# Second feed-forward layer of four batches: tokens sorted by expert in place of all experts for every token

## The chip, the cores and the metric

The kernel runs on one core of a Trainium2 chip. The metric is the device time of one execution in microseconds (us). Engines are named as in the profile: PE is the matrix engine (PEld its weight loads), DVE the vector engine, ACT the scalar engine, POOL the GpSimd engine, SP the engine that here only issues transfers. Everything is computed in f32.

## The reference, cut to what matters

```python
def ffn(x):                                  # x: tokens x 128
    scores = sigmoid(x @ gate_w.T)           # 16 experts
    _, idx = top_k(scores + gate_b, 4)
    w = take(scores, idx); w = w / w.sum(-1) * 2.5
    comb = zeros(T, 16).at[arange(T)[:, None], idx].add(w)
    y = sum(comb[:, e] * (silu_and_mul(x @ w13[e].T) @ w2[e].T) for e in range(16))
    return y + silu_and_mul(x @ w13_s.T) @ w2_s.T     # a shared expert, for every token

x = x + 0.5 * ffn(layernorm(x))
x = x + attention(layernorm(x))              # causal, rotary, one head of 128
x = x + 0.5 * ffn(layernorm(x))              # the same weights again
```

x has 8 batches of 1024 tokens of 128 features. An expert has 64 hidden units (gate and up halves of w13). Of 16 experts each token uses four; the weights in comb of the other twelve are zero.

## The kernel before, in words

The first feed-forward is layer 0, the second is layer 1. The unit of work is a `Group`: 512 tokens (half a batch) in one layer, 32 groups in all. A group computes all 16 experts for all its tokens: two experts make a block k of 128 hidden units, so there are eight blocks.

- Phase U, slots U0 to U8: for each k, `gate(k)` (line 273) and `up(k)` (286) are matmuls with 512 columns into PSUM banks that alternate; ACT applies SiLU (288), DVE multiplies by up (290) into `hidT`, and `weigh(k)` on POOL (294) multiplies by `cb`, the tokens' weights for the block's two experts.
- Phase D, slots D0 to D8: `down(k)` (302), four matmuls of 128 columns for each k, sums up the blocks; `down_shared` (311) adds the shared expert, whose hidden part `Shared.up` computed (336 to 341); `add` (317 to 325) adds half of it to x on DVE, and in layer 1 SP stores the result.

The order of the whole program is written by hand. A table `jobs` says, for every group's period p and each of its 18 slots, what else is put there; all engines get their instructions in that order, and each of them works through its own list in order. Beside group p's own U and D work, there stand in the slots of period p: the preparation of group p + 2 (`norm_a`, `norm_b`, `turn`, `route_a`, `route_b`, `score`, `top_a` to `top_c`: layer norm, transpose on PE, router, top four on DVE, lines 159 to 247), its `spread` (the weights go through DRAM, lines 256 to 266, and come back as `cb`, 2 MB a group, broadcast over 64 partitions), and the attention: for each batch `Heads` (norm, projections, rotary products on POOL, 376 to 394) and eight `Query` steps (`scores` 409, `exp` 420, `turn` 436 to 442, `attend` 448 to 452), two or three of them a period from period 3 to 28.

The group order interleaves the layers: layer 0 of batches 0 to 3, then layer 1 of batch b - 4 and layer 0 of batch b in turn, then layer 1 of batches 4 to 7.

PSUM has eight banks. Banks 0 to 3 serve U, bank 0 the sum of D; `hold` reserves banks for a stretch of slots, and `other_bank()` gives out the rest by age. Tiles in SBUF come from pools with so many buffers for each tag; a tile of which all buffers are in use makes its next writer wait.

Of the kernel before, what the change touches and what calls it, by code (L numbers as in the profile page):

```python
# [9 lines left out]
F32 = mybir.dt.float32  # L10
AF = mybir.ActivationFunctionType
# [4 lines left out]
P = 128  # L16
# [10 lines left out]
def kernel(  # L27
# [11 lines left out]
    rope: bass.AP,  # L39
    out: bass.AP,  # L40
# [16 lines left out]
    xpool = ctx.enter_context(tc.tile_pool(name="xpool", bufs=5))  # L57
    ln = ctx.enter_context(tc.tile_pool(name="ln", bufs=2))
    small = ctx.enter_context(tc.tile_pool(name="small", bufs=3))
# [35 lines left out]
    for n in range(2):  # L95
        bi = const.tile([P, GT, E + TOPK], F32, name=f"biased{n}")
        nc.gpsimd.memset(bi[:, :, E:], PAD)
        biased.append(bi)

# [47 lines left out]
    def stats(key, b, tiles):  # L147

        if key not in mvs:
            mvs[key] = small.tile([P, NT, 2], F32, tag="mv", name=f"mv_{key}", bufs=16)  # L150
        for t in tiles:
            st = small.tile([P, 6], F32, tag="st", name=f"st_{key}_{t}")
            nc.vector.bn_stats(st, xs[b][:, t, :])
            nc.vector.bn_aggr(mvs[key][:, t, :], st)

    def deviation(key, g):
        tiles = slice(g * GT, (g + 1) * GT)
        rstd = small.tile([P, GT], F32, tag="rstd", name=f"rs_{key}_{g}")
        nc.vector.tensor_scalar(rstd, mvs[key][:, tiles, 1], LN_EPS, None, ALU.add)
        nc.gpsimd.tensor_tensor(rstd, rstd, neg_half, ALU.pow)  # L160
        return rstd

    def normed(key, b, g, rstd):
        xn = ln.tile([P, GT, D], F32, tag=f"xn{key[0]}", name=f"xn_{key}_{g}")
        for j in range(GT):
            t = g * GT + j
            nc.vector.tensor_scalar(  # L167
                xn[:, j, :], xs[b][:, t, :], mvs[key][:, t, 0:1], rstd[:, j : j + 1],
                ALU.subtract, ALU.mult,
            )  # L170
        return xn
# [9 lines left out]
    class Group:  # L181
        def __init__(self, layer, b, g, n):
# [14 lines left out]
        def route_a(self):  # L197
# [7 lines left out]
            self.lt = small.tile([P, P], F32, tag="lt", name=f"lt_{self.nm}", bufs=2)  # L205
# [11 lines left out]
        def top_a(self):  # L217
# [3 lines left out]
            self.bi = biased[self.n % 2]  # L221
# [16 lines left out]
        def top_c(self):  # L238
# [3 lines left out]
            tot = small.tile([P, GT], F32, tag="tot", name=f"tot_{self.nm}")  # L242
# [9 lines left out]
        def spread(self, parts=2):  # L252
# [4 lines left out]
            cT = small.tile([P, P], F32, tag="cT", name=f"cT_{self.nm}", bufs=2)  # L257
# [3 lines left out]
            pairs = cd.rearrange("(n h) s -> h n s", h=2)  # L261
            self.cb = big.tile([P, NP, W], F32, tag="cb", name=f"cb_{self.nm}")
            for q in range(parts):
                ns = slice(q * NP // parts, (q + 1) * NP // parts)
                for h in range(2):
                    nc.sync.dma_start(
                        out=self.cb[h * I : (h + 1) * I, ns, :],
                        in_=pairs[h, ns, :].unsqueeze(0).broadcast_to([I, NP // parts, W]),
# [8 lines left out]
        def up(self, k):  # L277

            if k == 0:
                self.hidT = big.tile([P, NP, W], F32, tag="hidT", name=f"hidT_{self.nm}")  # L280
# [11 lines left out]
        def weigh(self, k):  # L292
            hid = self.hidT[:, k, :]
            nc.gpsimd.tensor_tensor(hid, hid, self.cb[:, k, :], ALU.mult)  # L294
# [32 lines left out]
    class Shared:  # L327
# [5 lines left out]
        def up(self):  # L333
            self.h = work.tile([P, W], F32, tag="sh", name=f"sh_{self.pair[0].nm}", bufs=1)
            for n, gr in enumerate(self.pair):
                nc.tensor.matmul(bank(5 - n), ws, gr.hT, start=True, stop=True)  # L336
            for n, gr in enumerate(self.pair):
                s_ps = bank(5 - n)
# [5 lines left out]
                gr.sh = self.h  # L344

    class Heads:
# [5 lines left out]
        def deviations(self):  # L354
# [5 lines left out]
            self.rl = small.tile([P, NT], F32, tag="rl", name=f"rl_{b}")  # L360
# [9 lines left out]
        def project(self, w, g):  # L370
# [4 lines left out]
            p = bank(5 - w)  # L375
# [3 lines left out]
            other = work.tile([P, W], F32, tag="ot", name=f"o_{nm}", bufs=2)  # L379
# [16 lines left out]
    class Query:  # L396
# [6 lines left out]
        def scores(self, first):  # L403
# [10 lines left out]
            top = self.top = small.tile([P, 1], F32, tag="top", name=f"top_{self.nm}")  # L414
# [3 lines left out]
        def exp(self):  # L418
            self.pr = att.tile([P, S], F32, tag="pr", name=f"pr_{self.nm}", bufs=3)
# [39 lines left out]
    LAG = 4  # L459
    order = [(0, b) for b in range(LAG)]  # L460
    for b in range(LAG, B):
        order += [(1, b - LAG), (0, b)]
    order += [(1, b) for b in range(B - LAG, B)]
# [4 lines left out]
    heads = [Heads(b) for b in range(B)]  # L468

# [7 lines left out]
    def when(p, slot):  # L477
        return p * len(slots) + slots.index(slot)

# [13 lines left out]
    queue = [(b, i) for b in range(B) for i in range(NT)]  # L493
    starts, done = {}, {}
    for p in range(3, 29):
        for n in range(2 if p in (15, 21) or (p % 2 == 0 and p != 26) else 3):
            if not queue:
                continue
            b, i = queue.pop(0)
            starts.setdefault(b, p)  # L500
            q = Query(heads[b], i)
            s, first, e, t0, t1, a = (
                ((p, "U7"), 4, (p, "D0"), (p, "D3"), (p, "D5"), (p, "D7")),
                ((p, "D2"), 2, (p, "D5"), (p, "D8"), (p + 1, "U0"), (p + 1, "U2")),
                ((p, "D4"), 4, (p, "D7"), (p + 1, "U3"), (p + 1, "U4"), (p + 1, "U5")),
            )[n]
            at(*s, lambda q=q, first=first: q.scores(first))
            hold((first, first + 1), s, e)
            at(*e, q.exp)
            at(*t0, lambda q=q: q.turn(0))  # L510
            at(*t1, lambda q=q: q.turn(1))
            at(*a, q.attend)
            done[b, i] = when(*a)
    assert not queue
# [3 lines left out]
    for b in range(B):  # L518
        h, st = heads[b], starts[b]
        ready = when(turn_of[0, b, 1] + 1, "U7")  # L520
        if b == 0:
            p0, p1 = st - 1, st - 1
            places = ("U8", "D0", "D2", "D3", "D5", "D6", "D7", "D8")
        else:
            p0, p1 = st - 2, st - 1
            places = ("D0", "D3", "D5", "D8", "U1", "U4", "U5", "U6")
        assert ready < when(p0, places[0])
        at(p0, places[0], h.deviations)
        at(p0, places[1], lambda h=h: h.norm(0))
        at(p0, places[2], lambda h=h: h.norm(1))  # L530
        at(p0, places[3], lambda h=h: h.turn(0))
        at(p1, places[4], lambda h=h: h.turn(1))
        for w in range(2):
            for p, slot, g in ((p1, places[5 + w], 0), (st, ("U4", "U5")[w], 1)):
                at(p, slot, lambda h=h, w=w, g=g: h.project(w, g))
                hold((5 - w,), (p, slot), (p, slot))
        at(p1, places[7], lambda h=h: h.values(0))
# [3 lines left out]
    for p, gr in enumerate(groups):  # L541
        steps = (
            gr.norm_a, gr.norm_b, gr.turn, gr.route_a, gr.route_b, gr.score, gr.top_a, gr.top_b,
            gr.top_c, gr.spread,
        )
        if p == 1:
            steps = steps[1:]
            places = [(0, s) for s in ("U3", "U5", "U6", "U8", "D0", "D1", "D2", "D3", "D6")]
        else:
            places = [(p - 2, s) for s in ("U5", "D1", "D4", "D5", "D7", "D7", "D8", "D8")]  # L550
            places += [(p - 1, "U1"), (p - 1, "U3")]
# [7 lines left out]
        if p % 2 == 0:  # L559
            pair = Shared(groups[p : p + 2])  # L560
            if p == 0:
                at(0, "D0", pair.up)
                at(0, "D3", gr.down_shared)
                hold((4, 5), (0, "D0"), (0, "D1"))
            else:
                jobs[p, "U0"] = [pair.up] + jobs.get((p, "U0"), [])
                hold((4, 5), (p, "U0"), (p, "U1"))
# [6 lines left out]

    for b in range(2, B):
        p = turn_of[0, b, 0]
        for g in range(NG):
            at(p - 4, "D8", lambda b=b, g=g: load_x(b, g))
            at(
                p + g - 3, "D6",  # L580
# [9 lines left out]
    def run(p, slot):  # L590
# [18 lines left out]
        lambda: gr0.spread(4), lambda: stats("f0_0", 0, range(GT, NT)), groups[1].norm_a,  # L609
# [105 lines left out]
```

## Time and profile before

| | |
|---|---|
| runs | 996.03, 996.43 and 997.23 us, median 996.43 |
| profiled execution | 997.42 us |
| its span in the trace | 995.6 us, granted clock 1.00 |
| POOL weighings (L294) | 256, mean 1.269 us |
| DVE gate products (L290) | 256, mean 0.687 us |
| ACT SiLU (L288) | 256, mean 0.597 us |
| ACT table loads | 62, each 1.283 us |
| bytes moved | 80.44 MB, mean 81 GB/s; queue q1 35.2% of 16 engines' span |
| `cb` loads | 124 of 512 KB, median 8.1 us from issue to landing |
| `x` loads | 16 of 256 KB, median 10.9 us |
| stores of the output | 15 of 256 KB, median 2.3 us |

A group row of the profile reads: source line, engine, operation, out<-in by tile names, shapes, xcount; then busy us and mean ns; then the idle time ahead of it and what ended most of it. A timeline row reads: start, length, engine, line, operation, xcount, and in brackets an idle time before it. A row of one tile gives minimum, median and maximum in ns. A row of a stretch gives the stretch, its length, the busy us of PE, PEld, DVE, ACT and POOL with instruction counts, the granted clock, the mean busy share of the 16 DMA engines and GB/s. A matmul in f32 leaves two records, a transpose one.

### The profile page before, as it was taken

To read this page: it belongs to the slowest core of one execution; us is meant where nothing else is said; L and a number is where in the kernel's file an instruction comes from. 1 tells how busy PE (TensorE), PEld (TensorE's weight loads), DVE (VectorE), ACT (ScalarE), POOL (GpSimd) and SP (SyncE) were. 2 spreads that over 40 slices of the span, in tenths; PEclk is the share of its full clock that TensorE was granted. 3 is DMA by queue.
4 is the path that set the end of the run, shared out by engine and by line. 5 is a ranking of instruction groups with operands and counts; after the bars stand their busy time and mean duration, and the time that the engine had idled before them with its cause. 6 is when DMAs were issued, how large, how long until landed. Compare 5 with 4: busy or idle time off the path is not lost.

```text
span 995.6 us, 14631 instructions
## 1 busy us (share of the span) xinstructions
PE 980.9 (99%) x5190; PEld 657.0 (66%) x5190; DVE 652.3 (66%) x2004; ACT 425.1 (43%) x766; POOL 450.3 (45%) x379
## 2 busy tenths in 40 slices
PE   8999999999999999999999999999999999999998
PEld 5656666776567666667566666767666766677665
DVE  6766787657766667756767666776667756664542
ACT  3334445443544445443544444444444444443331
POOL 2355555245633464335625365334644355423444
PEclk9999999999999999999999999999999999999999
DMA  5664333043413431245403443044321334134440
GB/s 161 161 121 106 87 86 86 3 107 86 87 43 65 108 87 41 57 97 107 87 19 80 95 108 80 10 95 97 86 66 39 80 87 95 43 67 92 92 97 21
DMA packets 56920, 80.44 MB, mean 81 GB/s; under 512 B 3600, under 2 KB 23440, under 8 KB 56720
## 3 DMA queue, kind: packets, MB, share of 16 engines
q1 hardware_dynamic: 55568, 78.26, 35.2%
q10 hardware_dynamic: 1280, 1.26, 0.4%
q8 instruction: 40, 0.66, 0.3%
q14 instruction: 32, 0.26, 0.1%
HBM read 74.27 MB, written 5.24 MB: 80 GB/s over the span
## 4 chain that ended last, share of the span: by engine, by line
PE 90%; DVE 7%; ACT 1%; issue 1%; POOL 0%; ACTq 0%; POOLq 0%; DVEq 0%
PE psum L302 23%; PE psum L273 20%; PE psum L286 19%; PE psum L409 6%; PE psum L448 6%; PE psum L436 3%; PE psum L311 3%; PE psum L376 3%; PE psum L176 2%; PE psum L336 2%; PE psum L390 1%; DVE sel L241 1%; PE psum L201 1%; DVE hidT L290 1%; PE psum L143 1%
## 5 line engine op out<-in xcount | busy, mean ns | idle before, releaser
L294 POOL TENSOR_TENSOR hidT<-hidT,cb 128x512 f32<-128x512 f32 x256 | 322.8, 1269 | 505.1 <-DVE hidT L290 316.7
L273 PE MATMUL psum<-hT,wg 128*128 128x512 f32 x512 | 262.2, 594 | 2.4 <-ACT sc L215 1.4
L286 PE MATMUL psum<-hT,wu 128*128 128x512 f32 x512 | 261.6, 592 | 0.0
L302 PE MATMUL psum<-wd,hidT 128*128 128x128 f32 x2048 | 255.9, 276 | 0.0
L302 PEld LDWEIGHTS psum<-wd,hidT 128*128 128x128 f32 x2048 | 242.3, 192 | 12.3 <-issue 10.3
L288 ACT ACTIVATE sg<-psum 128x512 f32<-128x512 f32 x256 | 151.9, 597 | 225.9 <-PE psum L273 210.8
L290 DVE TENSOR_TENSOR hidT<-psum,sg 128x512 f32<-128x512 f32 x256 | 175.3, 687 | 92.4 <-PE psum L286 86.1
L286 PEld LDWEIGHTS psum<-hT,wu 128*128 128x128 f32 x512 | 97.0, 190 | 122.7 <-issue 90.7
L273 PEld LDWEIGHTS psum<-hT,wg 128*128 128x128 f32 x512 | 88.3, 191 | 68.5 <-issue 55.9
L448 PEld LDWEIGHTS psum<-v,prT 128*128 128x128 f32 x576 | 72.4, 192 | 18.2 <-issue 16.3
L440 ACT COPY prT<-psum 128x512 f32<-128x512 f32 (+2 forms) x64 | 32.4, 506 | 112.9 <-PE psum L436 112.8
L448 PE MATMUL psum<-v,prT 128*128 128x128 f32 x576 | 74.7, 275 | 0.0
L409 PE MATMUL psum<-k,q 128*128 128x512 f32 (+2 forms) x192 | 72.5, 486 | 0.0
L167 DVE TENSOR_SCALAR xn_f<-x,mv_f,rs_f 128x128 f32<-128x128 f32 x128 | 68.9, 599 | 4.1 <-POOL rs_f L160 4.1
L321 DVE SCALAR_TENSOR_TENSOR x<-psum,x 128x512 f32<-128x512 f32 (+1 forms) x33 | 22.2, 674 | 64.7 <-PE psum L302 64.6
L413 DVE TENSOR_TENSOR psum<-psum,causal 128x128 f32<-128x128 f32 x64 | 19.1, 298 | 65.7 <-PE psum L409 65.3
L409 PEld LDWEIGHTS psum<-k,q 128*128 128x128 f32 x192 | 33.6, 191 | 27.7 <-issue 26.8
L415 DVE TENSOR_REDUCE top<-psum 128x1 f32<-128x128 f32 (+3 forms) x64 | 48.5, 758 | 2.2
L420 ACT ACTIVATE pr<-psum,top 128x128 f32<-128x128 f32 (+3 forms) x64 | 47.7, 745 | 0.3
L436 PE MATMUL psum<-ident,pr 128*128 128x128 f32 x288 | 46.5, 273 | 0.0
L311 PEld LDWEIGHTS psum<-wsd,sh 128*128 128x128 f32 x256 | 33.6, 192 | 14.8 <-issue 11.2
L436 PEld LDWEIGHTS psum<-ident,pr 128*128 128x128 f32 x288 | 35.1, 141 | 11.8 <-issue 11.8
(80 smaller groups left out, 973.3 us busy)
## 6 DMA issues: line engine op xcount, KB each, us to landing
cb<-cd SPq DMA_DIRECT2D x124, 512.0 KB, 8.1
x<-in_x SPq DMA_DIRECT2D x16, 256.0 KB, 10.9
out_x<-x SPq DMA_DIRECT2D x15, 256.0 KB, 2.3
cb<-cd SPq DMA_DIRECT2D x8, 256.0 KB, 5.7
cd<-cT SPq DMA_DIRECT2D x32, 32.0 KB, 1.8
cs<-in_rope SPq DMA_DIRECT2D x1, 1024.0 KB, 9.8
wg<-in_w_gate ACTq DMA_DIRECT2D x2, 256.0 KB, 6.2
wu<-in_w_up ACTq DMA_DIRECT2D x2, 256.0 KB, 5.9
```

What stands on the lines that cost most here:

```text
L167: nc.vector.tensor_scalar(xn[:, j, :], xs[b][:, t, :], mvs[key][:, t, 0:1], rstd[:, j : j + 1], ALU.subtract, ALU.mult,)
L273: nc.tensor.matmul(bank(2 * (k % 2) + 1), wg[:, units], self.hT, start=True, stop=True)
L286: nc.tensor.matmul(u_ps, wu[:, units], self.hT, start=True, stop=True)
L288: nc.scalar.activation(sg, g_ps, AF.Silu)
L290: nc.vector.tensor_tensor(hid, u_ps, sg, ALU.mult)
L294: nc.gpsimd.tensor_tensor(hid, hid, self.cb[:, k, :], ALU.mult)
L302: nc.tensor.matmul(self.y_of(j), self.hidT[:, k, j * P : (j + 1) * P], wd[:, k, :], start=(k == 0 and self.n == 0 and j == tiles[0]), stop ...
L311: nc.tensor.matmul(self.y_of(j), self.sh[:, j * P : (j + 1) * P], wsd[:, self.n % 2, :], start=(self.n > 0 and j == tiles[0]), stop=False,)
L409: nc.tensor.matmul(s[:, c:e], h.q[:, i * P : width], h.k[:, c:e], start=True, stop=True)
L415: nc.vector.tensor_reduce(top, s[:, :width], AX.X, ALU.max)
L436: nc.tensor.transpose(tp[:, j, :], self.pr[:, (k + j) * P : (k + j + 1) * P], ident)
L448: nc.tensor.matmul(o, self.prT[:, j, :], self.h.v[:, j, :], start=(j == 0), stop=(j == i))
```

## The change

Layer 1 of batches 0 to 3 is no longer computed as dense groups. Two chunks of two batches (2048 tokens, four `SortedGroup`s each) take their place, and the dense groups are 24: layer 0 of all eight batches in order (periods 0 to 15), then layer 1 of batches 4 to 7 (16 to 23).

- A `SortedGroup` does norm, transpose, router and top four as before, computes the shared expert at once, adds it to x and keeps x in DRAM (`kept`).
- `Chunk.count` and `places` find for each token and each of its four experts a row in a table of 80 tiles of 128 rows (64 tiles of choices and up to 16 for padding); each tile belongs to one expert, `owner`.
- `scatter`: 64 indexed transfers a chunk, issued by POOL, write the normalized rows (128 rows of 512 bytes each) to those places in DRAM. Ten plain transfers a chunk have written zeros there before.
- `Rows`: ten steps a chunk of eight tiles. A step loads eight experts' weights (128 KB each; the address comes from a register that SP loads from `owner`) and two sets of 512 rows, transposes them, multiplies with gate and up together, takes SiLU and product, multiplies with down, and stores the rows to `results` from ACT's queue.
- `gather`: 64 indexed transfers a chunk on POOL bring each token's four results back, and `gathered` on DVE adds each with its weight to x.

Places (period, slot): chunk 0 counts in period 8, scatters over 58 slots from (9, U0), runs `Rows` over 40 slots in 12 to 14 and gathers over 50 slots from (16, D2); chunk 1 counts in 12, scatters over 50 slots from (13, U0), runs `Rows` in 16 to 18 and gathers over 58 slots from (19, U8). Attention now has four queries a period in periods 3 to 18, in U slots too.

Further: `hidT`, `cT`, `lt` and other tiles have one buffer fewer, `ot` (the rotary product) shares the three buffers of `sg`, `cb` is loaded in two halves at two slots, projections and the shared part take any free bank, and in the last four groups DVE does every second `weigh`.

```diff
+        def gather(self, j, k):
+            if k == 0:
+                self.got[j] = sort.tile([P, TOPK, D], F32, tag="got", name=f"got_{self.nm}_{j}")
+            t = self.n * GT + j
+            nc.gpsimd.indirect_dma_start(
+                out=self.got[j][:, k, :], out_offset=None, in_=self.chunk.results,
+                in_offset=bass.IndirectOffsetOnAxis(ap=self.chunk.place[:, t, k : k + 1], axis=0),
+            )
+        def gathered(self, j):
+            t = self.n * GT + j
+            xt = self.x[:, j, :]
+            for k in range(TOPK):
+                nc.vector.scalar_tensor_tensor(
+                    xt, self.got[j][:, k, :], self.chunk.weight[:, t, k : k + 1], xt,
+                    ALU.mult, ALU.add,
+                )
...
+        def scatter(self, t, k):
+            nc.gpsimd.indirect_dma_start(
+                out=self.views[t * TOPK + k],
+                out_offset=bass.IndirectOffsetOnAxis(ap=self.place[:, t, k : k + 1], axis=0),
+                in_=self.groups[t // GT].xn[:, t % GT, :], in_offset=None,
+            )
...
+    class Rows:
+        def load(self):
+            self.x = []
+            for h in range(2):
+                q = 2 * self.i + h
+                x = sort.tile([P, GT, D], F32, tag="xs", name=f"xs{self.nm}_{h}")
+                nc.sync.dma_start(
+                    out=x,
+                    in_=self.chunk.rows[q * W : (q + 1) * W, :].rearrange("(t p) d -> p t d", p=P),
+                )
+                self.x.append(x)
+        def load_experts(self):
...
+                w = sort.tile([P, GT, 2 * D], F32, tag="wt", name=f"wt{self.nm}_{h}", bufs=4)
+                _, rows = nc.values_load_multi_w_load_instructions(
+                    self.chunk.owner[0:1, q * GT : (q + 1) * GT], engines=[mybir.EngineType.SP],
...
+                for j, row in enumerate(rows):
+                    nc.sync.dma_start(out=w[:, j, :], in_=w_table[bass.ds(row, D), :])
+        def up(self):
...
+                for j in range(GT):
+                    cols = slice(j * P, (j + 1) * P)
+                    nc.tensor.matmul(
+                        p[:, cols], self.w[h][:, j, :D], self.hT[h][:, cols], start=True, stop=True
+                    )
+                ss = work.tile([P, W], F32, tag="sg", name=f"sq{self.nm}_{h}")
+                nc.scalar.activation(ss[I:, :], p[:I, :], AF.Silu)
+                nc.vector.tensor_tensor(
+                    self.h[h * I : (h + 1) * I, :], p[I:, :], ss[I:, :], ALU.mult
+                )
+        def down(self):
...
+            for j in range(GT):
+                for h in range(2):
+                    rows, cols = slice(h * I, (h + 1) * I), slice(j * P, (j + 1) * P)
+                    nc.tensor.matmul(
+                        ps[h][:, cols], self.h[rows, cols], self.w[h][rows, j, D:],
+                        start=True, stop=True, tile_position=(h * I, 0),
+                    )
...
+            hid = self.hidT[:, k, :]
+            cb = self.cb[2 * k // NP][:, k % (NP // 2), :]
+            engine = nc.vector if self.n >= NPER - 4 and k % 2 else nc.gpsimd
+            engine.tensor_tensor(hid, hid, cb, ALU.mult)
...
-            other = work.tile([P, W], F32, tag="ot", name=f"o_{nm}", bufs=2)
+            other = work.tile([P, W], F32, tag="sg", name=f"o_{nm}")
...
+    SCATTER = (58, 50)
+    GATHER = ((18 * 16 + 11, 50), (18 * 19 + 8, 58))
+    SORTED = 2 * CB
+    order = [(0, b) for b in range(B)] + [(1, b) for b in range(SORTED, B)]
...
+        p = first + 3
+        at(p, "D7", chunk.count)
+        at(p, "D8", chunk.places)
...
+        n0 = when(p + 1, "U0")
+        for n in range(CT * TOPK):
+            at(*place_of(n0 + n * SCATTER[c] // 64), lambda chunk=chunk, n=n: chunk.scatter(n // TOPK, n % TOPK))
+        n1 = n0 + SCATTER[c] + 3
+        for i in range(NS // 8):
+            r = Rows(chunk, i)
+            m = n1 + 3 + 4 * i
+            at(*place_of(m - 5), r.load_experts)
+            at(*place_of(m - 3), r.load)
+            at(*place_of(m), r.turn)
+            at(*place_of(m + 1), r.up)
+            at(*place_of(m + 3), r.down)
```

## The prediction

> **What bounds the kernel now.** First the busy shares, then the chain that ended last, then PE's instructions in order of time for prices.
>
> ```profile
> PE 980.9 (99%) x5190; PEld 657.0 (66%) x5190; DVE 652.3 (66%) x2004; ACT 425.1 (43%) x766; POOL 450.3 (45%) x379
> ...
> PEclk9999999999999999999999999999999999999999
> ...
> PE 90%; DVE 7%; ACT 1%; issue 1%; POOL 0%; ACTq 0%; POOLq 0%; DVEq 0%
> ...
> L294 POOL TENSOR_TENSOR hidT<-hidT,cb 128x512 f32<-128x512 f32 x256 | 322.8, 1269 | 505.1 <-DVE hidT L290 316.7
> ```
>
> PE is the bound throughout, its granted clock is full, and nothing else is on the chain for long. POOL has 545 us to spare over the span. Prices are PE's start-to-start times, because busy times of pipelined matmuls overlap (timeline of PE; start, then length):
>
> ```profile
> 111.10 1.02 PE L286 MATMUL psum<-hT,wu 128*128 128x512 f32 x2
> 111.96 1.05 PE L311 MATMUL psum<-wsd,sh 128*128 128x128 f32 x8
> 112.85 2.84 PE L302 MATMUL psum<-wd,hidT 128*128 128x128 f32 x24
> ...
> 118.50 0.60 PE L176 MATMUL psum<-ident,xn_f 128*128 128x128 f32 x4
> 118.94 1.06 PE L302 MATMUL psum<-wd,hidT 128*128 128x128 f32 x8
> ```
>
> A matmul with 512 columns (two records) takes 111.96 - 111.10 = 0.86 us (0.857 over longer rows). Four of 128 columns (eight records) take 0.89, so 0.2225 each. Four transposes take 0.44, so 0.11. By the same reading 256 and 384 columns take 0.43 and 0.64, the four router matmuls 0.35.
>
> **PE's work.** Before, counted from the program: 624 of 512 columns (535 us), 1504 of 128 (335), 544 transposes (59), narrower scores 22, router 11: 962 us. The span's other 33.6 us are the start (first dense matmul at 9.7), the tail and short waits. After: 496 of 512 (425), 1248 full ones of 128 and the 160 expert matmuls of `Rows.up` (313), 696 transposes (75), scores 22, router 11, counting 2, and 160 `Rows.down` matmuls of only 64 rows. No row shows two 64-row matmuls on the two halves of the array: at full price 36 us, side by side 18; I take the middle, 27. Sum 876 (867 to 885): **86 us less**. A dense group costs 16 x 0.857 + 40 x 0.2225 and small things, 23.6 us; eight go (189), and 160 tiles, eight shared parts and 160 + transposes come back.
>
> **Where another engine is longer than PE.** The order is by hand, so PE waits in its place. I summed each engine's instructions between the first `wg` matmul of one dense group and the next (a period) with the mean durations of before. DVE's sums are multiplied by 0.913, since its groups add up to 714 us where it was busy 652. Periods 0 to 7 are PE's alone: in the others (us; c is POOL's time for one indirect transfer):
>
> | periods | PE | DVE | POOL |
> |---|---|---|---|
> | 8 | 42 | 47 | 19 + 2c |
> | 9-11 | 115.4 | 112 | 54 + 59c |
> | 12 | 50.7 | 52.5 | 19 + 5c |
> | 13-15 | 138.5 | 102 | 50.7 + 62c |
> | 16-18 | 147.3 | 115 | 45.7 + 57c |
> | 19-21 | 75.7 | 66 | 23.4 + 59c |
> | 22-23 | 43.5 | 24 | 10.3 + 12c |
>
> (POOL's constant: eight weighings of 1.27 us a period, four in the last four, powers of 1.01, rope products of 1.27.) Periods 8 and 12 hold `count` and `places`, some 35 dependent DVE instructions ahead of the next group's `hidT`: 4.9 + 1.8 us over PE, charged whole.
>
> **The open price, c.** No row of before is an indirect transfer. From below: SP issues a plain 256 KB store in 0.39 us. From above: 2.54, two of POOL's full tiles of 1.27 (one pass for each side of the transfer). Nearest are POOL's own two kinds of row, 1.01 us on 128x4 and 1.27 on 128x512; they hardly differ though one has 128 times the data, and a list of 128 rows lies between. I take **1.2**. POOL then exceeds PE by 9.4 us in 9-11 (54 + 70.8 against 115.4) and by 18.5 in 19-21; elsewhere PE hides it. With c = 0.39 both are nothing; with 2.54 the four stretches give 88 + 70 + 43 + 98 = 299.
>
> [...]
>
> **What the port does.** A DVE product of two SBUF tiles waits while POOL works:
>
> ```profile
> L241 DVE TENSOR_TENSOR sel<-sel,sc x32: 224/1260/1324, 13.9 to 951.3; 128x64 f32<-128x64 f32 x32
> L167 DVE TENSOR_SCALAR xn_f<-x,mv_f,rs_f x128: 327/337/1380, 6.9 to 939.4; 128x128 f32<-128x128 f32 x128
> ```
>
> Minimum, median, maximum in ns: `sel` nearly always waits out one weighing, of four consecutive `xn_f` about one does. The 128 new `gathered` additions come in fours; I price them like `xn_f`, 0.34 with one wait of 0.92 in four: 30 us more on DVE in periods 16-22, hidden (19-21: 66 + 14 under POOL's 94). If each waited: 19-21 has 66 + 59 x 0.94 = 121, 16-18 has 169, together 48 us above the bounds I use.
>
> [...]
>
> **The DMA queues.** One `Rows` step (eight tiles, four of a period's 18 slots, 11.7 us of PE in 13, 14, 16, 17) moves 0.52 MB of `xs`, 1.05 of `wt`, 0.52 of results, 0.47 of `cb`, 0.33 of scatter or gather: 2.9 MB. What full queues moved (share, GB/s at the end of each row):
>
> ```profile
> 206.00:211.00 5.00, 5.00 (x25) 3.09 (x24) 3.80 (x16) 2.61 (x5) 4.92 (x5) 1.00 1.07 222
> 211.00:214.00 3.00, 3.00 (x30) 3.00 (x29) 2.56 (x5) 1.11 (x3) 1.97 (x2) 1.00 1.15 205
> 6.00:10.00 4.00, 3.33 (x32) 2.89 (x32) 1.12 (x4) 2.03 (x3) 0.81 (x1) 1.00 1.09 341
> ```
>
> The first is `cb`, the second mostly `x` in 512-byte pieces (205 / 1.15 = 180), the third weights (341 / 1.09 = 313). `wt` at 313, `cb` at 208, `xs` at 180, the stores and indirect rows at 262 (0.26 MB of output in 284-286, 131 / 0.49): 3.4 + 2.2 + 2.9 + 3.3 = 11.8 us, as long as PE itself. Full queues land late, so I charge 0.4 us for each of 20 steps, **+8**. All at 180: 16.1, +88. All at 313: 9.3, nothing.
>
> **Other waits.** `ot` loses its two buffers and shares the three of `sg`: POOL's rope product and sum, 2.5 us behind one or two transfers of 1.2, now hold buffers that the next SiLU needs. Queued behind that SiLU on ACT are the following copies, and PE's gate matmul two steps on waits for its bank. Eight batches, at U4 and U5, 0 to 4 us each: I take **+8** (0 to 32). POOL's first scatter waits for `place`; behind it is only `weigh(0)`, whose `hid` comes later on DVE anyway. SP's queue: eight `wt` loads, two `xs` and two register loads per step; at 0.39 to 0.7 us an issue (rows of SP) 5 to 7 us, and the register loads, which no row shows, may take 2 us each before 11.7 are full; behind them wait `cd` and `cb`, due half a period later. `xs` is issued three slots ahead, some 8.5 us, where `x` took 10.9 to land behind 2 MB of `cb`, now in halves; that is in the +8. ACT's table loads go from 62 to 109 (1.28 us, +60), some between SiLUs: ACT's idle 570 us cover it; uncovered, 0.4 us at each of 16 places. The added POOL set-up at the start ends before its first power at about 6 us. Dropped buffers of `hidT`, `cT`, `lt` cost nothing while PE's order reads the old before it fills the new.
>
> **Sum.** 876 + 6.7 (periods 8, 12) + 27.9 (POOL) + 8 + 8 + 33.6 as before = span 960. The profiled execution took 997.4 on a span of 995.6, and the median of the runs is 1.0 below it: 960 + 1.8 - 1.0 = **961 us**.
>
> **Rivals.** (1) Transfers are cheap, c up to 0.9: PE alone decides, 876 + 6.7 + 33.6 + 0 to 16, about 925. For it: SP's 0.39. Against: no POOL row of use is below 1.0. (2) **POOL becomes the bound**, on the other side: c of 1.47 or more. Excess is 118c - 113.7 in 9-11 and 19-21 together, and from 1.42 also 62c - 87.8 in 13-15; the sum reaches 995.6 at c = 1.47. At 1.7: 39 + 48 + 18 = 105, so 1038. For it: POOL at 95% in those stretches already with 1.2; against: POOL's rows stop at 1.27. (3) Queues or port: all traffic at 180 GB/s gives 1041, every `gathered` waiting 1009. For it: the waits of `sel`; against: `xn_f`'s median. The change cannot fail to save its PE work: 160 tiles run whatever the routing.
>
> **Chances.** Forecast with c 1.0 to 1.4, 940 to 985: 0.45. Rival 1: 0.14. Rival 2: 0.26. Rival 3: 0.15, a fifth of it on the fast side. A measurement can tell 0.2% from no change: faster 0.62, same 0.03, slower 0.35. The range, 912 to 1065, leaves out c above 1.83 (0.11) and full hiding with both halves of the array side by side (0.04); the upper end of c alone would reach 1232 and is not taken in.
>
> **What would show it.** PE's busy sum by start times near 876; POOL's transfers near 1.2 us each and POOL 90% busy or more in periods 9-11 and 19-21, with `hidT` waiting for POOL on PE's `wd` line; PE the longest elsewhere. Transfers of 1.47 us or more, DMA share above 0.9 with PE waiting for `xs`, or `gathered` at 1.2 us each would prove a step wrong.

## The result, and the profile after

The changed kernel takes **1162.56 us** (median of four runs, 1161.07 to 1169.12) against 996.70 on the same chip: a ratio of 1.168, 95% interval 1.163 to 1.172. It is 166 us slower where 36 us faster was forecast, and above the range's end of 1065. The profiled execution has a span of 1161.6 us.

These lines of its page answer to those shown of before: busy times, PE by slices, its granted clock by slices, the chain that ended last, POOL's weighings.

```profile
PE 978.4 (84%) x5226; PEld 660.1 (57%) x5226; DVE 728.7 (63%) x2260; ACT 493.7 (43%) x822; POOL 605.6 (52%) x568
...
PE   8898999989995878778978688987988797876778
...
PEclk9999999999997889888989799998999898988998
...
PE 17%; POOL 7%; issue 6%; DVE 6%; DMA 4%; ACT 4%; another core or an unknown queue 2%; SPq 1%; ACTq 0%; POOLq 0%; DVEq 0%
...
L337 POOL TENSOR_TENSOR hidT<-hidT,cb 128x512 f32<-128x512 f32 x176 | 222.6, 1270 | 284.6 <-DVE hidT L331 221.4
```

No engine is full any more. PE was 99% busy and is 84%. The chain was 90% PE; its shares now add up to 47%, because the profile follows it back only to 610 us, and over that later part PE has about a third of it. POOL, which the forecast saw near its limit, is idle 221 us of the span waiting for DVE's `hidT`. And the clock row has eights and sevens: for 148 us behind the first gate matmul the granted clock was halved (before: none).

In the halved stretches a matmul takes twice its time (512 columns 1.71 us from start to start in place of 0.86, in the trace of e16, a second run of this kernel). PE was busy for 107 of the 148 us and idle in the rest, so the slow clock cost half of 107, 54 us, and PE's work at full rate is 978.4 - 54 = 925 us, against 980.9 before. PE's idle time (span less busy) went from 14.7 to 183.2 us: **-56 + 168 + 54 = +166**. PE's own work did fall; idle time and clock cost four times as much.

**Chips.** The experiments ran on five chips, called V to Z here; the kernel before took 996.4 to 996.9 us on each, but the changed kernel took 1162.6 on its own chip and 1108.4 on V (more on this at the end of the experiments), so that an edit is compared only with a kernel on the same chip, or between V and W, where no trace has the late signals told of there, though no kernel ran on both.

### The profile page after: what moved, and what is told of

Read it like the earlier page. It is cut to its first block, busy times and chain, and to the rows that moved or that the text cites. A ratio compares the mean times of both kernels' runs of the same rounds, so it can differ in the third digit from the quotient of the medians.

```text
span 1161.6 us, 16108 instructions
## 1 busy us (share of the span) xinstructions
PE 978.4 (84%) x5226; PEld 660.1 (57%) x5226; DVE 728.7 (63%) x2260; ACT 493.7 (43%) x822; POOL 605.6 (52%) x568
## 5 line engine op out<-in xcount | busy, mean ns | idle before, releaser
L337 POOL TENSOR_TENSOR hidT<-hidT,cb 128x512 f32<-128x512 f32 x176 | 222.6, 1270 | 284.6 <-DVE hidT L331 221.4
L327 PE MATMUL psum<-hT,wu 128*128 128x512 f32 x384 | 209.5, 629 | 24.2 <-DVE x L364 11.3
L314 PE MATMUL psum<-hT,wg 128*128 128x512 f32 x384 | 210.0, 630 | 18.9 <-DVE k L698 10.9
L345 PE MATMUL psum<-wd,hidT 128*128 128x128 f32 x1536 | 213.7, 289 | 12.3 <-issue 11.9
L345 PEld LDWEIGHTS psum<-wd,hidT 128*128 128x128 f32 x1536 | 197.5, 202 | 30.3 <-issue 26.6
L331 DVE TENSOR_TENSOR hidT<-psum,sg 128x512 f32<-128x512 f32 x192 | 131.2, 687 | 93.5 <-ACT sg L329 42.7
L450 POOL DMA_INDIRECT got<-results,place x128 | 124.8, 975 | 56.1 <-issue 28.4
L580 POOL DMA_INDIRECT rows<-xn_f,place x128 | 126.8, 990 | 50.5 <-issue 30.8
L459 DVE SCALAR_TENSOR_TENSOR xr<-got,wk,xr 128x128 f32<-128x128 f32 x128 | 56.3, 440 | 48.7 <-DMA got<-results,place 27.6
L633 PE MATMUL psum<-hTs,wt 128*128 128x128 f32 x320 | 44.3, 293 | 13.4 <-ACT hTs L624 9.1
```

What stands on the lines that cost most here:

```text
L314: nc.tensor.matmul(bank(2 * (k % 2) + 1), wg[:, units], self.hT, start=True, stop=True)
L327: nc.tensor.matmul(u_ps, wu[:, units], self.hT, start=True, stop=True)
L331: nc.vector.tensor_tensor(hid, u_ps, sg, ALU.mult)
L337: engine.tensor_tensor(hid, hid, cb, ALU.mult)
L345: nc.tensor.matmul(self.y_of(j), self.hidT[:, k, j * P : (j + 1) * P], wd[:, k, :], start=(k == 0 and self.n == 0 and j == tiles[0]), stop ...
L450: nc.gpsimd.indirect_dma_start(out=self.got[j][:, k, :], out_offset=None, in_=self.chunk.results, in_offset=bass.IndirectOffsetOnAxis(ap=s ...
```

## The experiments

My theory after the first trace (A): no engine is short of time; the sorted part's many steps stand in the lists of DVE, ACT and POOL ahead of what PE needs next, and PE, going through its own list in order, waits; the clock then makes it worse. The rivals: the attention, packed four queries to a period (B); POOL's transfers, by their time or by DVE's waits for POOL (P); the expert tiles' loads and short distances (R); later, too few PSUM banks.

**What each part costs (chip V).** Three kernels leave a part out or replace it. In e1 all that the loop over the chunks places is gone, and their rows go out as they are after the first layer:

```diff
     for c, chunk in enumerate(chunks):
-        first = 5 + 4 * c
...
         for m, gr in enumerate(chunk.groups):
+            at(5 + 4 * c + m, "U7", lambda gr=gr: keep(gr.b, gr.g))
```

In e2 the scatter (the gather alike, as a load into `got`):

```diff
-            nc.gpsimd.indirect_dma_start(
-                out=self.views[t * TOPK + k],
...
+            if k == 0:
+                nc.sync.dma_start(
+                    out=self.rows[n * P : (n + TOPK) * P, :].rearrange("(k p) d -> p k d", p=P),
+                    in_=self.groups[t // GT].xn[:, t % GT, :].unsqueeze(1).broadcast_to([P, TOPK, D]),
+                )
```

In e3 the steps of `Rows`, with `results` filled like `rows`:

```diff
-        for i in range(NS // 8):
-            r = Rows(chunk, i)
...
+            nc.sync.dma_start(
+                out=self.results[part * n : (part + 1) * n, :].rearrange("(p a) d -> p a d", p=P),
+                in_=zeros.unsqueeze(1).broadcast_to([P, n // P, D]),
+            )
```

> Leaves out the whole second layer of batches 0 to 3 (normalising, routing, counting, scatter, expert tiles, gather); their rows after the first layer are stored as output. What stays is the dense groups and the attention in the changed order: by the prices of the prediction PE's work is 876 - 21 (eight sorted groups at 2.65) - 81 (expert tiles) - 2 = about 773 us. Theory A (the sorted steps that stand in the in-order queues cost the idle time of PE): with them gone PE idles little more than before, the clock stays full, span 800 to 830. Theory B (the attention, four queries a period, half of them beside the gate and up matmuls, costs it): PE still idles 4 to 8 us in each of 13 periods and the clock falls now and then, span 860 to 900.

> Each set of four scatters becomes one plain store of a tile four times over, each set of four gathers one plain load, both from SP, to and from consecutive rows; so the rows of each expert tile are not those of its expert, and the output is not the reference's. The 256 indirect transfers are gone from POOL, everything else stays. Theory A (DVE's and ACT's order, not POOL): PE's idle time and the slow clock stay, 1120 to 1165. [...]

> Leaves out the expert tiles (loads, transposes, both matmuls, stores); the results that the gathers read are filled with zeros by ten more stores. PE's work falls by about 81 us to 795. Theory R (the expert tiles' waits, for their loads and for the copies and products between their matmuls, cost the idle time of periods 13, 14 and 16 to 18): those periods fall back to their PE work, which takes away 81 us of work and some 75 of the 95 us that they ran over it: about 1000 to 1020. Theory A without them (any step in the queues costs, the clock falls anyway): only the work goes, 1065 to 1090.

Measured, one run each: e1 828.2 us, e2 1048.8, e3 1018.0. The changed kernel itself was run on this chip later:

> The changed kernel itself, unaltered, on the same chip as the two that follow. Between the calls so far the traces differ in one thing: in some calls every kernel with indirect transfers has gaps of 1 to 17 us in which PE's semaphore updates come late (7 to 21 such gaps a run, 21 to 112 us of them, in the changed kernel 7 with 23 us), in others none has any. If this goes by chip and not by kernel, the changed kernel comes out either near 1162 with such gaps, or, without them, near 1110, as the one with later scatters or own ot buffers did. If it goes by kernel, it has the same seven gaps and 1160 to 1165 on any chip, while the next has none.

It took **1108.4 us** (four runs, 1103.2 to 1115.5), 1.112 of before (1.107 to 1.118). So the loss goes by chip in part, and this is the number to compare with. The engines' rows of e16, e1, e2 and e3, and of e17, which comes below:

```profile
PE 956.4 (86%) x5226; PEld 648.1 (59%) x5226; DVE 731.4 (66%) x2260; ACT 494.2 (45%) x822; POOL 606.0 (55%) x568
```
```profile
PE 796.3 (96%) x4230; PEld 533.3 (65%) x4230; DVE 521.9 (63%) x1732; ACT 394.6 (48%) x678; POOL 344.5 (42%) x304
```
```profile
PE 937.1 (89%) x5226; PEld 640.0 (61%) x5226; DVE 713.4 (68%) x2260; ACT 494.7 (47%) x822; POOL 353.2 (34%) x312
```
```profile
PE 871.3 (86%) x4426; PEld 571.0 (56%) x4426; DVE 695.9 (68%) x2180; ACT 427.4 (42%) x726; POOL 606.5 (60%) x568
```
```profile
PE 962.4 (88%) x5226; PEld 654.6 (60%) x5226; DVE 729.3 (67%) x2262; ACT 497.0 (45%) x824; POOL 605.0 (55%) x568
```

The same sums by run, the last five on chip V (us). "Idle" is span less busy, "half" the time at half rate behind the first gate matmul, "busy in it" what PE was busy of that, and PE's work is its busy time less half of "busy in it"; so the span is work, idle time and half of the last column:

| kernel | span | PE's work | idle | half | busy in it |
|---|---|---|---|---|---|
| before (first chip) | 995.6 | 981 | 15 | 0 | 0 |
| changed (first chip) | 1161.6 | 925 | 183 | 148 | 107 |
| e16, changed | 1107.5 | 919 | 151 | 102 | 75 |
| e1, dense groups alone | 826.4 | 793 | 30 | 8 | 7 |
| e2, no indirect transfers | 1047.0 | 916 | 110 | 65 | 43 |
| e3, no expert tiles | 1016.2 | 835 | 145 | 102 | 72 |
| e17, spread counting | 1095.6 | 920 | 133 | 96 | 85 |

- e1 is a hit for theory A: the dense groups and the attention in their new order keep PE 96% busy. The packed attention is not the cause; the sorted part is, which takes 281 us for 126 us of PE's work.
- e2 lies in theory P's band as written (1000 to 1060), but both bands were reckoned from 1162. Moved down by the 54 us between the chips they are 1066 to 1111 for A and 946 to 1006 for P, and 1048.8 lies in neither. Against 1108.4 the transfers on POOL are worth 60 us (41 of idle time, 16 of clock, 3 of work), with the same DMA bytes. They take 250 us of POOL's time, and DVE's busy time falls by 18 without them, so that DVE's waits for POOL explain at most some 18 of the 60. POOL is not full either (55%). What is left is order: what stands behind a transfer on POOL comes late. That is argued from what is left over; the runs below that move the transfers do not confirm it.
- e3 takes away 91 us, of which 84 are work and 6 idle time. Theory R falls: without the tiles PE idles nearly as long, so that their waits, where there are tiles, stand in place of other waits. (As written the number 1018 agreed with R alone, by the wrong reference; moved down by 54, A's band of 1011 to 1036 holds it and R's of 946 to 966 does not.)

By stretches between first gate matmuls, e16 over e1: periods 5 to 8 +39 us, 9 to 12 +63, 13 to 18 +136, 19 to 23 +45. In 19 to 23 no PE work was added at all (609 PE records in both; e2 over e1: +19 us): only gathers on POOL and `gathered` on DVE. POOL was 75% busy in periods 9 to 11 of e16 and 73% in 19 to 21 (114.7 of 152.1 and 82.4 of 113.0 us).

**Where an in-order queue makes PE wait.** The counting of chunk 0, in period 8 of e16. PE first, then DVE (start, length, engine, line, operation; in brackets the idle time before it):

```profile
347.00 1.06 PE L706 MATMUL psum<-wqkv,hT_a 128*128 128x128 f32 x8
357.56 0.61 PE L559 MATMUL psum<-ident,ows 128*32 128x128 f32 x2 [9.51 <-DVE ows L540]
362.62 2.07 PE L314 MATMUL psum<-hT,wg 128*128 128x512 f32 x2 [4.45 <-DVE owner_i L561]
```
```profile
344.25 0.69 DVE L698 TENSOR_TENSOR q<-psum,cs 128x512 f32<-128x512 f32 x1 [1.61 <-ACT o_q L697]
...
350.83 0.67 DVE L698 TENSOR_TENSOR k<-psum,cs 128x512 f32<-128x512 f32 x1
...
351.87 2.70 DVE L500 TENSOR_TENSOR sums<-sums 128x256 f32<-128x256 f32 x4
...
357.23 0.18 DVE L540 TENSOR_SCALAR ows<-owner 128x32 f32<-128x32 f32 x1
...
360.84 1.31 DVE L552 MAX8 top<-at 128x8 f32<-128x16 f32 x16
...
362.29 0.27 DVE L561 TENSOR_SCALAR owner_i<-psum 1x128 int32<-1x128 f32 x1
```

PE runs into a small matmul (L559) whose operand is the end of DVE's chain, 9.5 us away; the gate matmul then gets the bank that L559 wrote, and its reader `owner_i` stands on DVE behind another group's top four and 16 maxima: 4.5 us more. DVE works without a pause up to there: over the period of 58.9 us it is busy for 47.1, but there is no time to spare here. PE's list of waits in e16 (us, times, longest) is many such meetings, none large:

```profile
PE psum L623 <- DMA xs<-rows: 17.2, 7, 4.7
PE psum L559 <- DVE ows L540: 14.4, 2, 9.5
PE psum L209 <- DVE xn_f L200: 12.6, 4, 5.5
PE psum L327 <- DVE hidT L331: 11.9, 13, 2.3
PE psum L314 <- DVE k L698: 10.9, 2, 5.8
PE psum L291 <- DVE comb L282: 10.4, 7, 3.6
PE psum L327 <- DVE x L364: 9.5, 3, 5.8
PE psum L380 <- ACT pr L736: 7.0, 6, 1.2
```

**What an idle stretch does to the clock.** The same place in stretches of 3.41 us (columns: stretch, length, busy us of PE, PEld, DVE, ACT, POOL with counts, granted clock, DMA share, GB/s):

```profile
349.72:353.13 3.41, 0.00 (x0) 0.00 (x0) 3.34 (x8) 0.00 (x0) 1.26 (x1) 0.61 0.01 2
353.13:356.55 3.42, 0.00 (x0) 0.00 (x0) 3.11 (x11) 0.00 (x0) 0.00 (x0) 0.50 0.00 0
356.55:359.96 3.41, 0.61 (x2) 0.18 (x2) 3.17 (x15) 0.00 (x0) 0.00 (x0) 0.50 0.00 0
359.96:363.37 3.41, 0.75 (x1) 0.50 (x2) 2.46 (x29) 0.00 (x0) 0.69 (x1) 0.50 0.00 0
363.37:366.79 3.42, 3.42 (x7) 1.60 (x6) 0.07 (x1) 1.88 (x2) 1.51 (x2) 0.50 0.13 41
366.79:370.20 3.41, 3.41 (x18) 2.40 (x17) 2.04 (x8) 0.60 (x1) 2.28 (x2) 0.89 0.02 5
```

The clock is halved from 350.5 to 367.6 us, five windows of 3.413 us, the last of them with PE already full: in these rows the rate of a window goes by how busy PE was in the one before (the counts stand in the last section). In e16 there are 30 such windows; PE was busy for 75 us of them, which cost 37.

**Mends.** The counting cut into steps and spread, with the scatters eight slots later, L559 far behind its operand:

```diff
-        at(p, "D8", chunk.places)
+        for n, f in enumerate((chunk.count_b, chunk.count_c, chunk.count_d)):
+            at(p + 1, f"U{n + 1}", f)
+        for m in range(CT // GT):
+            at(p + 1, f"U{m + 4}", lambda chunk=chunk, m=m: chunk.places(m))
+        at(p + 1, "D6", chunk.tile_owners)
...
-        n0 = when(p + 1, "U0")
+        n0 = when(p + 1, "U8")
```

> The same computation; the counting is cut into four steps in U1 to U3 of the next period and the places into four more in U4 to U7, the scatters start eight slots later, and the small matmul that turns the tiles' owners round is issued in D6 of that period rather than right behind the DVE chain it reads. If waits for the chain of DVE instructions cost the time of periods 8 and 12 and the start of 9 (9.5 + 4.5 + 4.8 us of gaps, and the slow clock after them, 9.3 + 8.8 us of windows at half rate): 25 to 35 us less, 1128 to 1138. If the time is given back elsewhere (the later scatters, the chain now ahead of hidT in the U slots): within 8 us of 1162.

> The kernel with the spread counting, unaltered, beside the changed kernel on the same chip. If the counting's chain is worth what its gaps and half-rate windows show: 15 to 35 us under the changed kernel here. If its 70 us were all its own: 65 to 75 under it. If they were the chip's: within 8 us.

1091.9 us at first, 1096.5 (1087.4 to 1105.9) beside the changed kernel's 1108.4: 12 to 16 us, at or just under the lower end of the second text's band. Periods 8 and 12 shorten by 11 and 10 us and 16 by 10; 18 and 14 lose 13 and 6 again. The 70 us that the first comparison seemed to give were mostly the chip's.

Chip W, where no run has the late signals told of below: own buffers for `ot` (e8; with the spread counting e9 and e11), the later `n0` alone (e10), and slots without transfers (e11):

```diff
-            other = work.tile([P, W], F32, tag="sg", name=f"o_{nm}")
+            other = work.tile([P, W], F32, tag="ot", name=f"o_{nm}", bufs=2)
...
+            rope = ("U4", "U5", "U6", "D6", "D7", "D8")
+            free = [m for m in range(first, first + span) if place_of(m)[1] not in rope]
+            return [free[n * len(free) // 64] for n in range(CT * TOPK)]
```

> The changed kernel with two buffers of their own for ot, the rope's tile, as before the change (paid for by one buffer less of the normalised rows and of the transposed tiles). The prediction charged 8 us (0 to 32) for the shared ring. If the shared ring (a SiLU that waits for a buffer which POOL's rope product still holds behind transfers) is a main cause: 1100 to 1135. If not: 1150 to 1165.

> The kernel with the spread counting (1091.9), with the two buffers for ot besides. Ring theory: 1040 to 1070. Otherwise within 10 us of 1092.

> The changed kernel with one number altered: the scatters, and all that follows them but the gathers, begin eight slots later (U8 in place of U0 of the period after the counting); counting stays one chain. This splits the 70 us of the spread counting. If the chain is what cost: little, 1140 to 1160. If POOL's first weighings, standing behind scatters that wait for their places, or the meeting of steps in the slots cost: 1100 to 1125.

> The spread counting with own ot buffers, and no transfer issued in U4 to U6 and D6 to D8, where POOL makes the rope products that queries and keys wait for; the same transfers in the other slots of the same stretches. If POOL's short jobs that stand behind transfers are what costs (the D slots alone made it 144 us slower, with these jobs behind 14 transfers): 20 to 40 us under the run with own ot buffers. If only the total on POOL counts: within 8 us of it.

1112.4, 1097.4, 1111.4 and 1104.7 us. Against 1108.4 and 1092 to 1097 on chip V, own buffers for `ot` give nothing, nor do later scatters alone; e9 under e8 is the spread counting again, 15 us. Keeping the rope's slots free of transfers made it 7 us slower (e11 over e9, two runs each). The ring theory falls, and so does the simple form of the queue theory, that the rope products are what stands behind the transfers.

**On other chips**, over the spread counting: a bank kept for the gate matmul (e5, e7) and transfers in D slots alone (e6, e7) on chip X; loads and stages further apart on Y (e12). The lines, in this order:

```diff
+        hold((1,), (p, "D6"), (p, "D8"))
...
+        def d_slot(first, n):
+            return when(first + n // 18, f"D{n % 18 // 2}")
...
-            m = n1 + 3 + 4 * i
-            at(*place_of(m - 5), r.load_experts)
-            at(*place_of(m - 3), r.load)
+            m = n1 + 3 + 5 * i
+            at(*place_of(m - 6), r.load_experts)
+            at(*place_of(m - 4), r.load)
```

> The kernel with the spread counting, and bank 1 kept from other steps from D6 to D8, so that the first gate matmul of the next group does not wait for the DVE product of a key projection. If that wait is worth what its gaps show (3.5 + 5.8 + 5.0 + 2.7 us before the gate matmul, and the half-rate windows behind them): 12 to 25 us under the kernel with the spread counting (1091.9), so 1067 to 1080. If the product only makes the next step late instead (fewer banks for the same steps): within 6 us of 1092.

> The kernel with the spread counting, and the 256 indirect transfers issued in D slots alone, two a slot, where no weighing stands behind them on POOL; their number and time stay. If POOL costs by its queue (a weighing, and so the down matmuls, behind a transfer): about half of what taking the transfers off POOL gave (114 us from the changed kernel), so 1030 to 1060. If it costs by its total time or by the port: 1080 to 1100.

> Both: bank 1 kept and the transfers in D slots alone, over the spread counting. If the causes are separate waits of the in-order queues: the two gains add up (within 10 us). If all of it is one shortage (DVE and ACT simply have too much), the second gain is under half of its size alone.

> The spread counting (1091.9), with the expert tiles' steps five slots apart in place of four, their loads and their three stages each a slot further apart (load four slots ahead of the transposes, matmuls two and four behind), and the gathered sums three slots behind their transfers in place of two; the same work in all. If late loads and the short distances between the stages of one expert step cost the time of periods 13 to 18 (13 to 21 us over PE's work in four of them, 18 us of gaps named for the loads of the rows): 1050 to 1075. If what costs is that any step's DVE and ACT instructions stand in line with those of the others, wherever they are put: 1080 to 1105.

1160.2, 1235.5, 1239.7 and 1147.1 us, all far off. The spread counting was not run on these chips, so e5 and e12 decide nothing by themselves. Within chip X, the D slots cost 75 us (e6 over e5), with the same transfers and POOL busy 602 us against 605. So where the transfers stand counts on this chip, not how many there are; but e6's trace has some 60 us more of the late signals told of below than e5's, so that most of the 75 goes with them, and what long runs of transfers cost without late signals was not run. The bank changes nothing (e7 over e6: +4).

Chip Z tested PSUM banks: in slots U1 to D0 of some periods only two banks are free, for up to 24 uses. Scores hold what they need (e13, e15, e18), or the expert tiles leave the U slots (e14, e15):

```diff
-        hold((first, first + 1), s, e)
+        hold((first, first + 1)[: 1 + i // GT], s, e)
...
-            m = n1 + 3 + 4 * i
+            a = 10 * c + i
+            m = when(13 + a // 3, f"D{a % 3 * 3}")
```

> The spread counting (1091.9); scores of at most 512 columns hold one PSUM bank in place of two, so that in the odd periods from 3 to 17 the steps of slots U1 to D0 take turns in three banks and not in two (the program has 19 to 24 such steps in those slots of periods 13, 14, 17 and 18, and 8 to 11 in the other periods). Bank theory (PE waits for the DVE or ACT instruction that reads the bank before its next use, and with two banks that is the one just before): periods 11, 13 and 17 shorten, 1055 to 1080. Rival (the DVE and ACT queues are late whatever the banks): within 8 us of 1092.

> The spread counting; the twenty steps of expert tiles in D slots alone (three a period, transposes, first and second matmuls in consecutive slots, from period 13 to 19), where five banks and not two are free; two more buffers for the rows' tiles, one less for normalised rows and for transposed ones. Bank theory: 1045 to 1075. Rival (DVE and ACT stand in line, and nine D slots now hold all of it): 1090 to 1130.

> Both edits: expert tiles in D slots alone and only the banks that the scores need. Bank theory: the best of the runs that compute all, 1030 to 1065. Rival: as the expert tiles in D slots alone, within 8 us.

> The spread counting with only the PSUM banks that the scores need, unaltered, beside the other two. On another chip than the spread counting it was 50 us slower. Bank theory: 12 us or more under the spread counting here. Rival (the banks do not matter, the 50 us were the chip's): within 8 us of it.

1142.2, 1165.9 and 1162.2 us on chip Z; on chip V, beside the spread counting's 1096.5, 1090.6 (1082.0 to 1095.6). With banks to spare the tiles in D slots gain 4 us from them (e15 under e14), the U slots 6 on chip V, where the runs overlap; expert tiles in D slots alone lose 20 (e15 over e13), on a chip with late signals. The bank theory falls: its 12 us and more are not there. That DVE and ACT are late whatever the bank is what remains, and was not shown by a run of its own. e18, at 1.096 of before (1.093 to 1.099), is the fastest kernel here that computes all. No version beat the one before.

**What differs between the chips.** In the changed kernel's own trace SP's instructions for the `wt` loads, then the same on chip V (ns, minimum, median, maximum):

```profile
L614 SPq MOVE wt<-in_w_table x160: 2/29/707, 544.3 to 926.2; - x160
L614 SPq DMA_DIRECT2D wt<-in_w_table x160: 4/333/1396, 544.4 to 926.3; - x160
```
```profile
L614 SPq MOVE wt<-in_w_table x160: 29/29/38, 524.2 to 887.6; - x160
L614 SPq DMA_DIRECT2D wt<-in_w_table x160: 332/333/1107, 524.3 to 887.7; - x160
```

A register move of 29 ns took up to 707. PE in the same stretch of the changed kernel's own trace:

```profile
649.22 0.50 PE L345 MATMUL psum<-wd,hidT 128*128 128x128 f32 x3 [0.92 <-issue]
650.65 0.49 PE L209 MATMUL psum<-ident,xn_f 128*128 128x128 f32 x3 [0.93 <-issue]
652.07 0.37 PE L209 MATMUL psum<-ident,xn_f 128*128 128x128 f32 x1 [0.94 <-issue]
659.88 1.01 PE L633 MATMUL psum<-hTs,wt 128*128 128x128 f32 x3 [7.44 <-ACT hTs L624]
```

It stops 0.9 us after every three records with nothing to wait for, and the semaphore updates of what it had finished by 652.4 are recorded from 652.8 to 659.5; DVE, which waits for them, goes on at 654.9 and ACT at 659.2. POOL alone does not stop: it issued 14 scatters back to back from 639.3 to 656.8 us. The changed kernel's own trace has seven to nine such gaps with late updates, 23 to 29 us by the way of counting; e6 has 16 to 21 (92 to 110 us), e7 21 or 22 (112 to 127); e5, e12 and e13 to e15 have 7 to 13 (21 to 45). Every kernel on V and W has none, nor has before. Nearly all of those in the changed kernel come in or just behind a run of four or more back-to-back transfers, but equal runs on V and W go with none.

The traces with late updates also lack records: in the changed kernel's own, about 60 of PE's 1198 semaphore updates, 50 of ACT's 595 and 110 of DVE's 1710 are missing, and none of POOL's. On V and W no engine lacks more than five. So the recording of the run loses data on those chips, and the stops may belong to the recording; whether an execution that is not recorded has them, no run here shows.

Of the changed kernel's 166 us, 54 go with the chip (idle 183 against 151 us, 107 against 75 us busy at half rate), and 112 are there without any late signal. What the chips differ in was not found.

## Why the prediction was wrong, point by point

- **PE's work, -86.** About right. At full rate the busy time falls by 62 us on chip V and by 56 in the own trace. It counts the end of the last matmul before each pause, 0.16 us (a record of 128 columns is 0.27 long, the next starts 0.11 later), and there are 108 and 137 busy stretches in place of 20; without these ends it falls by some 75 (an estimate from these numbers). The 64-row matmuls run side by side (see the last section): 18 us, not the middle 27.
- **The price c, 1.2.** Right: 0.96 us and 0.30 to the next, 1.26 from start to start.

```profile
643.12 1.01 POOL L580 DMA_INDIRECT rows<-xn_f,place  x1 [0.30 <-issue]
644.43 0.96 POOL L580 DMA_INDIRECT rows<-xn_f,place  x1 [0.30 <-issue]
645.70 0.96 POOL L580 DMA_INDIRECT rows<-xn_f,place  x1 [0.30 <-issue]
```

- **POOL, +27.9.** The term from this price was mis-sized: 60 us on chip V (e2), though POOL is not the bound: 75% and 73% busy where 90% or more was forecast. The likely reason, which no run shows by itself: a sum over three periods lets POOL catch up within them; PE, in its place in the list, cannot wait for that without losing time.
- **Counting, +6.7.** 12 to 16 (e17, e4). DVE's sum was right in period 8 (47.1 us busy, 47 forecast), but the period took 58.9: the chain stands right ahead of a matmul, which the sum cannot see, and the clock is halved behind it.
- **`ot`, +8.** Nothing that these runs can tell (e8, e9).
- **Queues, +8.** Not separated. PE's waits for `xs` are 17 us in e16, 9 in e2 with the same bytes; e12, which gave the loads more time, ran on a chip without a reference. DVE's waits for POOL, which the prediction calls the port: before, 29 of 32 `sel` took 1.25 us or more, each until 0.08 us behind the end of one of POOL's products; in the changed kernel 5 of the 24 of the dense groups took over 1 us. `gathered` took 0.44 us on the mean, less than the price (0.34 with one wait of 0.92 in four is 0.57).
- **"The remainder, 33.6 as before".** This step failed: "elsewhere PE hides it". It took every period in which no other engine's sum is longer as PE's own, at full clock. PE's idle time is 151 us instead (e16), e1's 30 with the sorted part's 121 on top, plus 37 of clock, which no term and no rival had. Of the 121, e2 accounts for 41 and e17 for 18; about 60 were not separated, and their cause stays open. Candidates are the sorted groups' routing in D slots (periods 5 to 7, +20 us for some 8 of work), `gathered` in 19 to 23 (e2 is 19 over e1 there), and what expert steps add to both.
- **Rivals.** Rival 2 had the right sign and the wrong mechanism: c stayed under its 1.47 and POOL is 52% busy. Rival 3 is not seen either: DVE's waits for POOL explain at most some 18 us, and PE's waits for `xs` are 17. The one that the runs point to, in-order lists that meet at the wrong places, had a lump of 8 us for `ot`; it is shown for the counting alone.

The loss on the first chip beyond 1108 could not be read from the trace of before, which has no indirect transfer.

## What to carry to other kernels

Where the kernel before keeps one engine full, price not only the sums of a change but each place where the full engine's next instruction reads something from the end of another engine's list: DVE was 66% busy and still made PE wait. Idle stretches cost more here than their length: in e16 the 75 us for which PE was busy in windows at half rate cost 37. And compare edits on one chip, with the unaltered kernel beside them: 54 us of a first "gain" of 70 went with the chip.

## What the runs showed of the hardware

- **The clock.** Windows of 3.413 us on a fixed grid. Over all kernels here, behind a full-rate window in which PE was busy 41% or less, the next was at half rate every time (325 windows); behind one of 62% or more never (5026); in between, in 78 of 292. In the changed kernel's own trace it was 19 windows of 19, none of 253, and 5 of 21. Before the change no window was under 55%. So 2 us of idle time in one full-rate window (59% of 3.413), in one piece or several, were enough every time in these traces.
- **Two 64-row matmuls** on the two halves of the array run at once: in the changed kernel's own trace the starts of 133 of the 160 pairs are 6 to 7 ns apart, and at full rate the next pair follows 0.11 us later. Eight of them (16 records) and eight full ones in the changed kernel's timeline:

```profile
668.15 1.16 PE L647 MATMUL psum<-wt,hs 64*128 64x128 f32 x16
...
674.16 2.05 PE L633 MATMUL psum<-hTs,wt 128*128 128x128 f32 x16 [1.68 <-ACT hTs L624]
```

- **Indirect transfers** of 128 rows hold POOL 0.95 us (the medians are 0.96 for scatters and 0.95 for gathers), and never over 1.27 in the changed kernel.
- **Late signals**, as told above, on some chips, with runs of such transfers: seven to nine gaps of 23 to 29 us in all in the changed kernel's own trace, none on V and W. Why some chips have them, no run here shows.
